# Layer 1 of a four-layer network: where y starts, who adds the scan's steps, and who applies the third norm's factor

## The chip, the cores and the metric

The kernel runs on one core of one Trainium2 chip. The metric is the device time of one launch in microseconds (us), the median of several runs. A core has a matrix engine (PE, TensorE), a vector engine (DVE, VectorE), an activation engine (ACT, ScalarE), a general engine (POOL, GpSimd) and a queue engine (SP) that here issues DMAs. They run beside each other, and each works through its own instructions strictly in the order in which the program lists them.

## The reference

An input of 16 images, 96 channels, 56 x 56 pixels (L = 3136) goes through four layers. Layer 0 is a masked convolution block; layers 2 and 3 are Fourier mixers with an MLP. The change touches layer 1 alone, a selective scan over the image in four directions:

```python
u = _ln(z, norm1_g, norm1_b) @ in_proj_w.T
uc = silu(depthwise_conv3x3(u))                      # 192 channels
xs = [rows, columns, rows reversed, columns reversed] # of uc
dts, Bs, Cs = split(einsum('bkdl,kcd->bkcl', xs, x_proj_w))
dt = softplus(dt_projs_w @ dts + dt_projs_b)
a  = exp(dt * A);  bb = dt * Bs * xs
h  = scan(h = a * h + bb)                            # along L, in each direction
y  = h * Cs + Ds * xs
ym = sum of the four directions, turned back into the image
z  = z + _ln(ym, out_norm_g, out_norm_b) @ out_proj_w.T   # second norm
m  = _ln(z, norm2_g, norm2_b)                             # third norm
z  = z + gelu(m @ fc1_w.T + fc1_b) @ fc2_w.T + fc2_b
```

## The kernel before

Layer 1 is the function `layer1`. For each image it has six generators (L1495 to L1530), which run as tasks beside each other for different images:

- `normed` (L1065) and `front` (L1097): first norm, projection into 192 channels, the 3 x 3 convolution as matmuls with diagonal taps into PSUM tiles `p_c` (L1170), eviction by ACT (L1191), Silu (L1193), the small projection `p_x` (L1207). The 192 channels of an image lie in two tiles of 128 partitions: `u0` holds the first 128; `um` holds the other 64 twice, once by rows and once by columns.
- `made_of` (L1220): for twelve units per image (six combinations of tile and direction, two halves each) and two steps of 784 columns per unit, PE makes `p_d` (L1237), ACT turns it into `dt` (exponential L1244, logarithm L1246) and `a` (exponential, L1253). `rows_of` loads the rows of B and C, spread over partitions, as `bc` (L1266).
- `scanned` (L1274): per step of 784 columns, DVE multiplies `dt` by `u` (L1325) and by B into the PSUM tile `driven` (L1328), scans (`TENSOR_TENSOR_SCAN`, L1334 backward and L1336 forward), and, one step later in `finish`, multiplies the state by C into `hc` (L1289). For units 0 and 2, the first of each tile, DVE then starts the output, `y = dsum * u + hc` (L1292). For the other four units GpSimd adds `hc` to y (L1358), in `sums` (L1341). In the end DVE adds the turned half of `ym` to the other (L1363).
- `back` (L1368): statistics of y and the second norm, then for seven groups of 448 pixels: output projection, DVE's `z` (L1428, L1432), squares on ACT (L1438), sums on DVE (L1440 to L1443), GpSimd's power -1/2 giving the third norm's factor `r` (L1445), DVE's product `zn = z * r` (L1447), transposition on PE (L1451), then the MLP (L1461, L1463, L1471) and the sum (L1474). Three chains of groups run side by side.

The order of each engine's queue is not written by hand. Each generator yields an `Op` with an engine and a cost before it issues that piece of work, and `in_order` (L276) plays all tasks against modelled engines: of all waiting pieces it issues the one with the lowest start time plus a lead. The leads stand in `TUNED` by engine and generator; an ACT piece that needs another function table also gets `hold` added. A piece can take buffers (`take`), free them (`give`), wait for a time that another has posted, and post one. Which piece follows which thus comes from the costs, leads and buffer counts; on the chip the order is then fixed. What an `Op` covers is issued in one piece, such as the nine taps of a convolution block:

```python
yield pe(9, 0.66, ())
for k in range(9):
```

The tiles `u0`, `um` and the two y of an image come from a list of seven (`big`).

Of the kernel before, what the change touches and what calls it, by code (L numbers as in the profile page):

```python
# [23 lines left out]
T = 448  # L24
NT = L // T
ROWS = T // S
Q = 112
# [32 lines left out]
def packed(x):  # L60
# [96 lines left out]
    for m in (C, DIN):  # L157
# [21 lines left out]
                        'z': 2,  # L179
                        'zn': 1,  # L180
                        'zt': 1,
                        'hid': 1,
                        'xr': 2},
            'leads': {('PE', 'spreads'): -2.2,
                      ('PE', 'steps'): -3.4,
                      ('SP', 'sums'): -1.2,
                      ('ACT', 'spreads'): -0.3,
                      ('DVE', 'additions'): -0.2,
                      ('ACT', 'hidden'): -0.7,
                      ('SP', 'norms'): 0.7,  # L190
                      ('POOL', 'fronts'): -4.6,
                      ('DVE', 'some'): -0.3,
                      ('POOL', 'norms'): 0.4,
                      ('PE', 'some'): -0.6,
                      ('ACT', 'sums'): 0.5,
                      ('SP', 'projected'): -1.4,
                      ('DVE', 'norms'): 0.1,
                      ('POOL', 'backs'): -0.6,
                      ('POOL', 'additions'): -1.3,
                      ('PE', 'projected'): 0.7,  # L200
                      ('DVE', 'backs'): -1.8,
                      ('ACT', 'fronts'): -0.2,
                      ('PE', 'fronts'): -2.4,
                      ('DVE', 'spreads'): -0.8,
                      ('SP', 'rows_of'): 0.2},
            'hold': 0.7,
            'norm': -6,
# [679 lines left out]
def layer1(ctx, tc, src, given, dst, flags=None, soft=False):  # L887
# [151 lines left out]
    def pe(n, each, take=("ps",), give=(), **k):  # L1039
        return Op("PE", 1.05 * n * each, 0.25, take, give, **k)  # L1040

# [55 lines left out]
    def front(b, it):  # L1097
# [60 lines left out]
        def convolved(j):  # L1158

            pad, u = (whole, halves)[j], us[j]  # L1160
            for c in range(0, (8, 4)[j], 2):
                yield Op("none", 0.0, 0.0, take=("ps",))
                p = pair("p_c")
                yield pe(9, 0.66, ())
                for k in range(9):
                    for b in range(2):
                        r0 = 7 * (c + b) + k // 3
                        for s in range(2):
                            to = (s ^ b) * 64
                            nc.tensor.matmul(  # L1170
                                p[to : to + 64, b, :TC], taps[64 * s : 64 * s + 64, j, k],
                                pad[64 * s : 64 * s + 64, r0 : r0 + 7, k % 3 : k % 3 + S],
                                start=k == 0, stop=k == 8,
                            )
                at = TC * c
                if j == 0:
                    outs = [
                        (u[:, at : at + TC], p[:, 0, :TC], TC),
                        (u[:64, at + TC : at + 2 * TC], p[64:, 1, :TC], TC),
                        (u[64:, at + TC : at + 2 * TC], p[:64, 1, :TC], TC),  # L1180
                    ]
                else:
                    outs = []
                    for s, b in ((0, 0), (0, 1), (1, 0), (1, 1)):
                        to, row = (s ^ b) * 64, HALF_S * s + 7 * (c + b)
                        own = p[to : to + 64, b, :TC]
                        outs.append((u[:64, S * row : S * row + TC], own, TC))
                        outs.append((turned(u[64:])[:, row : row + 7], own.rearrange("p (h w) -> p h w", w=S), 1.7 * TC))
                for i, (out, in_, cost) in enumerate(outs):
# [11 lines left out]
        for b in range(2):  # L1201
            yield pe(3, 0.7, ("ps",) if b == 0 else ())
            p = pair("p_x") if b == 0 else p
# [16 lines left out]
    def made_of(it):  # L1220
# [4 lines left out]
        def steps():  # L1225

            for unit in units:
                i, h = unit
                order = (0, 1) if i < 3 else (1, 0)
                for s in order:  # L1230
# [11 lines left out]
                    else:  # L1242
                        yield act(SUB, give=("ps",), table="exp")
                        nc.scalar.activation(flat, p[:, :, :TC], AF.Exp, bias=dtb[:, i : i + 1])  # L1244
                        yield act(SUB, table="exp")
                        nc.scalar.activation(dt, dt, AF.Ln, bias=one)  # L1246
# [3 lines left out]
                for s in order:  # L1250
                    give = ("proj",) if last and s == order[1] else ()
                    yield act(SUB, give=give, table="exp", post=times[unit, s])
                    nc.scalar.activation(a[:, SUB * s : SUB * s + SUB], made[unit][s], AF.Exp, scale=aneg[:, i : i + 1])  # L1253
# [20 lines left out]
    def scanned(it):  # L1274
# [4 lines left out]
        def scan():  # L1279
            y0, ym = None, None  # L1280
            before, late = None, None

            def finish(unit, s, a, t, end, out, own_u):
                i = unit[0]
                yield dve(
                    SUB, take=("hc",), give=("bc",) + (("a",) if end else ()), post=None if i in (0, 2) else added[unit, s]
                )
                made[unit]["hc", s] = hc = buf([P, SUB], "hc")
                nc.vector.tensor_tensor(hc, a, t[:, 1], ALU.mult)  # L1289
                if i in (0, 2):  # L1290
                    yield dve(SUB, give=("hc",), post=added[unit, s])
                    nc.vector.scalar_tensor_tensor(  # L1292
                        out, own_u, dsum[:, i // 2 : i // 2 + 1], hc, ALU.mult, ALU.add
                    )

            for unit in units:
# [3 lines left out]
                u = um if mixed else u0  # L1300
                if unit in ((0, 0), (2, 0)):
                    yield Op("none", 0.0, 0.0, take=("big",))
                    y = big.pop(0)
                    if mixed:
                        ym = y
                    else:
                        y0 = y
                    it["y"].append(y)
                y = ym if mixed else y0
                for s in ((1, 0) if back else (0, 1)):  # L1310
# [9 lines left out]
                    free = end and i in (4, 5)  # L1320
                    yield dve(SUB, 1.85e-3 if flip else 1.04e-3, wait=times[unit, s], give=("big",) if free else ())
                    if free:
                        big.append(u)
                    dt, a = made[unit][s], made[unit]["a"][:, SUB * s : SUB * s + SUB]
                    nc.vector.tensor_tensor(as_own(dt), as_own(dt), own(u), ALU.mult)  # L1325
                    yield dve(SUB, wait=bct[unit, s], give=("dt",))
                    t, b = bcs[unit, s][0], driven[:, :SUB]
# [9 lines left out]
                    before = None if end else (a[:, 0:1] if back else a[:, SUB - 1 : SUB], last_sub)  # L1337
                    late = (unit, s, a, t, end, own(y), own(u))
            yield from finish(*late)

        def sums():  # L1341
            for unit in units:
                i, h = unit
                back = i >= 3
                if i in (0, 2):
                    continue
                for s in ((1, 0) if back else (0, 1)):
                    at = HALF * h + SUB * s
                    yield Op("none", 0.0, 0.0, wait=added[unit, s])
                    y, u = it["y"][i == 5], (um if i == 5 else u0)  # L1350
                    hc = made[unit]["hc", s]
# [3 lines left out]
                    else:  # L1355
                        out = y[:, at : at + SUB]
                    yield Op("POOL", 1.9, give=("hc",))
                    nc.gpsimd.tensor_tensor(out, out, hc, ALU.add)  # L1358
            ym = it["y"][1]
            for g in range(4):  # L1360
                yield dve(L / 4, 1.85e-3)
                own = image(ym[:64])[:, 14 * g : 14 * g + 14]
                nc.vector.tensor_tensor(own, own, turned(ym[64:])[:, 14 * g : 14 * g + 14], ALU.add)  # L1363

        it["sums"] = sums()
        yield from scan()

    def back(b, it):  # L1368
# [38 lines left out]
        def group(g):  # L1407
# [16 lines left out]
            for q in range(4):  # L1424
                nc.tensor.matmul(p[:Q, 4 + q, :C1], each(x, q), rows[0], start=True, stop=True)
            yield dve(4 * C1, take=("z",))
            z = buf([Q, 4, C1], "z")
# [15 lines left out]
            nc.vector.tensor_scalar(v, v, 1.0 / C, EPS, ALU.mult, ALU.add)  # L1443
            yield Op("POOL", 1.4)
            nc.gpsimd.tensor_tensor(r, v, nhalf[:, :4], ALU.pow)  # L1445
            yield dve(4 * C)
            nc.vector.tensor_tensor(zn, z, r.unsqueeze(2).to_broadcast([Q, 4, C]), ALU.mult)  # L1447
            yield pe(4, 0.1, ("ps", "zt"), ("zn",))
# [9 lines left out]
            def hidden(j):  # L1458
                yield pe(1, 0.75, ("ps",), ("zt",) if j == 2 else ())
                p = pair("p_f")  # L1460
                nc.tensor.matmul(p[:, 0, :T], w_fc1[:, P * j : P * j + P], zt, start=True, stop=True)  # L1461
                yield act(T, table="gelu", give=("ps",))
                nc.scalar.activation(hid[:, j], p[:, 0, :T], AF.Gelu, bias=b_fc1[:, j : j + 1])  # L1463
# [22 lines left out]
    def item():  # L1486
        lists = lambda: {(k, s): [] for k in units for s in range(2)}
        return {
            "y": [], "left": NT, "ready": [], "normed": [], "done": [], "begun": [], "made": {k: {} for k in units},
            "times": lists(), "bcs": lists(), "bct": lists(), "added": lists(),  # L1490
        }
# [472 lines left out]
```

## Time and profile before

| | |
|---|---|
| median of 3 runs | 7093.66 us (7093.59 to 7100.32) |
| profiled execution, its own time | 7093.59 us |
| its span in the profile | 7091.7 us |
| layer 1 in it | 1152.6 to 4401.8 us |
| busy in layer 1 (3249.2 us) | PE 2708.5, DVE 2618.9, ACT 2320.4, POOL 948.7 us |
| L1292, all of it (DVE) | 128 instructions, 132.2 us |
| L1447, all of it (DVE) | 112 instructions, 142.5 us |
| L1358, all of it (POOL) | 256 instructions, 528.3 us |

In the profile, a group's line gives the source line, engine, operation, output and inputs with shapes, the count, then the busy time and the mean length in ns of one, then how long the engine was idle just before such instructions and for whom it waited. A timeline line begins with the start and the length in us, and ends with the idle time in brackets. PEclk is the share of its full clock that PE was granted.

### The profile page before, as it was taken

The numbers are of one execution on the slowest core, as the hardware profiler recorded it, in microseconds if no ns is written. First come the engines' busy times: TensorE is split into PE (matmuls) and PEld (weight loads), VectorE is DVE, ScalarE is ACT, GpSimd is POOL, SyncE is SP. The second block draws the span as 40 slices with busy tenths as digits, with TensorE's granted clock in tenths as the row PEclk, the third lists the DMA queues.
The fourth block names the chain that finished last, engine by engine and source line by source line (L and its number), as shares of the span: only waits on it lengthen the run. The fifth ranks groups of instructions, "written<-read, shape, count | busy, mean of one in ns | idle before, by whom it ended". The sixth has DMA issues, their size and how long they took to land. (4 is left out here: it accounts for less than half of the span.)

```text
span 7091.7 us, 113066 instructions
## 1 busy us (share of the span) xinstructions
PE 6092.5 (86%) x45643; PEld 4183.4 (59%) x45643; DVE 5440.8 (77%) x7075; ACT 4521.6 (64%) x5897; POOL 1377.5 (19%) x898
## 2 busy tenths in 40 slices
PE   7999997888888888888888866788999989999986
PEld 3444443345445455555544444787888888888875
DVE  6786884598888888888888894667777777777775
ACT  4454542677777777777777762455666666666664
POOL 0000000233332323233332231111111111111110
PEclk9999997788898898888888867899999999999997
DMA  1111111444444444444544342445555455555542
GB/s 38 32 38 34 38 33 52 132 143 134 131 137 132 136 133 138 130 138 135 140 131 126 110 128 64 97 107 123 130 116 128 111 130 119 123 134 118 120 105 62
DMA packets 508374, 763.72 MB, mean 108 GB/s; under 512 B 206337, under 2 KB 339137, under 8 KB 504530
## 3 DMA queue, kind: packets, MB, share of 16 engines
q1 hardware_dynamic: 506818, 753.53, 41.2%
q8 instruction: 363, 5.95, 0.4%
q0 software_dynamic: 1024, 2.85, 0.1%
q14 instruction: 169, 1.38, 0.1%
HBM read 563.65 MB, written 192.59 MB: 107 GB/s over the span
## 5 line engine op out<-in xcount | busy, mean ns | idle before, releaser
L1664 POOL TENSOR_TENSOR r<-v,nhalf 112x16 f32<-112x16 f32 (+1 forms) x128 | 392.9, 3076 | 2238.8 <-DVE v L1662 1677.2
L1358 POOL TENSOR_TENSOR big<-big,hc 128x784 f32<-128x784 f32 x256 | 528.3, 2064 | 1139.4 <-DVE hc L1289 1131.3
L1325 DVE TENSOR_TENSOR dt<-dt,big 128x784 f32<-128x784 f32 x384 | 500.6, 1304 | 249.4 <-ACT a L1253 249.1
L827 DVE SCALAR_TENSOR_TENSOR h<-pad,rows,h 128x1568 f32<-128x1568 f32 x288 | 525.9, 1844 | 3.9
L1244 ACT ACTIVATE dt<-p_d,l_dtb 128x784 f32<-128x784 f32 x384 | 350.3, 912 | 183.0 <-PE p_d L1237 157.8
L1237 PE MATMUL p_d<-proj,l_dt 32*128 32x392 f32 x1536 | 382.8, 581 | 93.5 <-ACT big L1191 52.4
L1461 PE MATMUL p_f<-zt,w_fc 96*128 96x448 f32 x672 | 401.7, 731 | 41.9 <-ACT zt L1454 27.8
L1471 PE MATMUL p_g<-l_fc,hid 128*112 128x96 f32 x2688 | 425.5, 304 | 11.7 <-ACT hid L1463 11.0
L1722 PE MATMUL p<-k_f,z 112*128 112x112 f32 x3072 | 375.0, 282 | 67.5 <-DMA z<-d 57.9
L1722 PEld LDWEIGHTS p<-k_f,z 112*128 112x128 f32 x3072 | 370.6, 199 | 76.3 <-issue 57.9
L1471 PEld LDWEIGHTS p_g<-l_fc,hid 128*112 128x112 f32 x2688 | 385.4, 219 | 41.0 <-ACT hid L1463 30.8
L1770 PE MATMUL p_v<-w,gg 128*112 128x97 f32 x2048 | 377.9, 267 | 34.5 <-DVE gg L1759 11.6
L1170 PE MATMUL p_c<-x,taps 64*64 64x392 f32 x4608 | 400.8, 497 | 0.8 <-ACT big L1191 0.8
L1328 DVE TENSOR_TENSOR drive<-dt,bc 128x784 f32<-128x784 f32 x384 | 387.8, 1010 | 10.2
L1771 PE MATMUL p_v<-w2both,gg 128*112 128x97 f32 x2048 | 376.0, 266 | 0.0
L1289 DVE TENSOR_TENSOR hc<-a,bc 128x784 f32<-128x784 f32 x384 | 371.8, 968 | 3.4 <-POOL big L1358 3.4
L1246 ACT ACTIVATE dt<-dt,one 128x784 f32<-128x784 f32 x384 | 363.4, 946 | 8.5
L1691 PE MATMUL p_a<-first,xt 97*112 97x192 f32 x1792 | 336.6, 336 | 18.1 <-ACT xt L1685 9.0
L1334 DVE TENSOR_TENSOR_SCAN a<-a,drive 128x784 f32<-128x784 f32 x192 | 350.3, 1825 | 0.0
L1336 DVE TENSOR_TENSOR_SCAN a<-a,drive 128x784 f32<-128x784 f32 x192 | 350.2, 1824 | 0.0
L1253 ACT ACTIVATE a<-dt,aneg 128x784 f32<-128x784 f32 x384 | 347.5, 937 | 2.7 <-DVE a L1334 1.4
L800 PE MATMUL p_c<-pad,taps 64*64 64x392 f32 x4032 | 347.4, 494 | 0.3 <-ACT pad L782 0.3
(341 smaller groups left out, 14838.7 us busy)
## 6 DMA issues: line engine op xcount, KB each, us to landing
bc<-bc SPq DMA_DIRECT2D x256, 784.0 KB
bc<-bc SPq DMA_DIRECT2D x256, 392.0 KB
d<-y SPq DMA_DIRECT2D x448, 192.0 KB
z<-d SPq DMA_DIRECT2D x128, 672.0 KB
d<-uu SPq DMA_DIRECT2D x256, 169.8 KB
z<-d SPq DMA_DIRECT2D x192, 194.0 KB
xc<-x SPq DMA_DIRECT2D x96, 336.0 KB
x<-in_x SPq DMA_DIRECT2D x16, 1176.0 KB
```

The lines of the kernel that those rows point to most:

```text
L827: nc.vector.scalar_tensor_tensor(out, view, taps9[:, i : i + 1], out, ALU.mult, ALU.add)
L1170: nc.tensor.matmul(p[to : to + 64, b, :TC], taps[64 * s : 64 * s + 64, j, k], pad[64 * s : 64 * s + 64, r0 : r0 + 7, k % 3 : k % 3 + S], s ...
L1237: nc.tensor.matmul(p[:, b, :TC], wdt[on, i], proj[on, h], start=True, stop=True)
L1325: nc.vector.tensor_tensor(as_own(dt), as_own(dt), own(u), ALU.mult)
L1328: nc.vector.tensor_tensor(b, dt, t[:, 0], ALU.mult)
L1358: nc.gpsimd.tensor_tensor(out, out, hc, ALU.add)
L1461: nc.tensor.matmul(p[:, 0, :T], w_fc1[:, P * j : P * j + P], zt, start=True, stop=True)
L1471: nc.tensor.matmul(p[:Q, q, :C], hid[:, j, own], fc2[:, j], start=j == 0, stop=False)
L1664: nc.gpsimd.tensor_tensor(r, v, nhalf[:, :n], ALU.pow)
L1722: nc.tensor.matmul(p[:, q, :Q], flat[:, P * (3 * q + k) : P * (3 * q + k) + P], f2, start=True, stop=True)
L1770: nc.tensor.matmul(out, gs[2 * h][:, at + k], w["w2"][:, 2 * h], start=True, stop=False)
L1771: nc.tensor.matmul(out, gs[1][:, at + k], w["w2both"][:, h], start=False, stop=True)
```

## The change

Five things change in `layer1`, and with them the planned order of all queues:

- y begins as `dsum * u` on ACT: four new instructions of 1568 columns per image, in a new generator `inits` that runs beside the scan. The first tile's y is made at the start, the second's after a step of unit 4. The count `uses` decides when a `u` tile returns to the list.
- DVE's L1292 goes; GpSimd adds `hc` for all six units instead of four.
- The taps of a convolution block are announced to the planner in three pieces of three.
- The third norm's factor is applied to z by GpSimd, behind its power, and `zn` has two buffers.
- Costs, leads and `hold` (0.7 to 0.0) of the planner have other values.

```diff
-                        'zn': 1,
+                        'zn': 2,
...
-            'leads': {('PE', 'spreads'): -2.2,
+            'leads': {('PE', 'spreads'): -0.9,
                       ('PE', 'steps'): -3.4,
-                      ('SP', 'sums'): -1.2,
+                      ('SP', 'sums'): 1.2,
...
-                      ('POOL', 'fronts'): -4.6,
+                      ('POOL', 'fronts'): -6.6,
...
-                      ('PE', 'fronts'): -2.4,
...
+                      ('ACT', 'inits'): 0.7,
+                      ('PE', 'hidden'): -2.0,
+                      ('POOL', 'some'): -0.9,
...
-            'hold': 0.7,
+            'hold': 0.0,
...
     def pe(n, each, take=("ps",), give=(), **k):
-        return Op("PE", 1.05 * n * each, 0.25, take, give, **k)
+        return Op("PE", 1.1 * n * each, 0.25, take, give, **k)
...
                 p = pair("p_c")
-                yield pe(9, 0.66, ())
                 for k in range(9):
+                    if k % 3 == 0:
+                        yield pe(3, 0.66, ())
...
                 nc.vector.tensor_tensor(hc, a, t[:, 1], ALU.mult)
-                if i in (0, 2):
-                    yield dve(SUB, give=("hc",), post=added[unit, s])
-                    nc.vector.scalar_tensor_tensor(
-                        out, own_u, dsum[:, i // 2 : i // 2 + 1], hc, ALU.mult, ALU.add
-                    )
...
         def sums():
             for unit in units:
                 i, h = unit
                 back = i >= 3
-                if i in (0, 2):
-                    continue
                 for s in ((1, 0) if back else (0, 1)):
                     at = HALF * h + SUB * s
                     yield Op("none", 0.0, 0.0, wait=added[unit, s])
+                    yield Op("none", 0.0, 0.0, wait=it["begins"][i in (2, 5), h])
...
-                    yield Op("POOL", 1.9, give=("hc",))
+                    yield Op("POOL", 2.1, give=("hc",))
                     nc.gpsimd.tensor_tensor(out, out, hc, ALU.add)
...
+        def inits():
+            for j, u in enumerate((u0, um)):
+                if j:
+                    yield Op("none", 0.0, 0.0, wait=added[(4, 1), 1])
+                yield Op("none", 0.0, 0.0, take=("big",))
+                y = big.pop(0)
+                it["y"].append(y)
+                for h in range(2):
+                    yield act(HALF, post=it["begins"][j, h])
+                    cols = slice(HALF * h, HALF * h + HALF)
+                    nc.scalar.activation(y[:, cols], u[:, cols], AF.Identity, scale=dsum[:, j : j + 1])
+                it["uses"][j] -= 1
+                if it["uses"][j] == 0:
+                    big.append(u)
+                    yield Op("none", 0.0, 0.0, give=("big",))
+
         it["sums"] = sums()
-        yield from scan()
+        yield [scan(), inits()]
...
-            yield Op("POOL", 1.4)
+            yield Op("POOL", 1.6)
             nc.gpsimd.tensor_tensor(r, v, nhalf[:, :4], ALU.pow)
-            yield dve(4 * C)
-            nc.vector.tensor_tensor(zn, z, r.unsqueeze(2).to_broadcast([Q, 4, C]), ALU.mult)
+            yield Op("POOL", 1.1)
+            nc.gpsimd.tensor_tensor(zn, z, r.unsqueeze(2).to_broadcast([Q, 4, C]), ALU.mult)
```

## The prediction

> **What bounds the kernel now.** I began with the 40 slices of the page, to find the stage that the change touches.
>
> ```profile
> PE   7999997888888888888888866788999989999986
> DVE  6786884598888888888888894667777777777775
> ACT  4454542677777777777777762455666666666664
> POOL 0000000233332323233332231111111111111110
> PEclk9999997788898898888888867899999999999997
> ```
>
> A slice is 177 us. Slices 8 to 24 are layer 1 (first instruction at 1152.6 us, last at 4401.8): PE and DVE both stand at 8 of 10, ACT at 7, POOL at 2 or 3. Nobody is full, so averages won't tell. The timeline shows DVE beginning the scans of an image every 190.4 us (1834.4, 2024.8, 2215.9, 2404.4, 2594.8 ...). I cut one such period in two where the second of DVE's two long waits ends, and asked for busy times by window:
>
> ```profile
> 2403.90:2464.80 60.90, 51.38 (x565) 22.93 (x562) 40.18 (x41) 51.58 (x67) 12.10 (x14) 0.92 0.33 109
> 2464.80:2594.30 129.50, 112.47 (x701) 71.18 (x699) 123.02 (x138) 94.38 (x118) 46.68 (x26) 0.87 0.53 147
> ```
>
> Columns: length, then busy us of PE, weight loads, DVE, ACT, POOL, then clock, DMA share and GB/s. The halves have different limits. **Part A** (60.9 us, the convolution of the next image): DVE 66%, PE and ACT 84 and 85%. **Part B** (129.5 us, most of the scans beside norms, projections and the MLP): DVE 95%, PE 87%, ACT 73%. So B is DVE's, and A belongs to PE and ACT feeding each other. Next the groups and waits of ten periods (1834.4 to 3738.3; divide by ten):
>
> ```profile
> L1325 DVE TENSOR_TENSOR dt<-dt,big 128x784 f32<-128x784 f32 x240 | 314.0, 1308 | 163.3 <-ACT a L1253 163.3
> L1447 DVE TENSOR_TENSOR zn<-z,r 112x384 f32<-112x384 f32 x70 | 93.9, 1342 | 13.2 <-POOL r L1445 13.2
> L1292 DVE SCALAR_TENSOR_TENSOR big<-big,dsum,hc 128x784 f32<-128x784 f32 x80 | 82.6, 1033 | 2.1
> L1358 POOL TENSOR_TENSOR big<-big,hc 128x784 f32<-128x784 f32 x160 | 329.1, 2057 | 715.6 <-DVE hc L1289 713.4
> L1445 POOL TENSOR_TENSOR r<-v,nhalf 112x4 f32<-112x4 f32 x70 | 111.3, 1590 | 376.2 <-DVE v L1443 375.4
> L1451 PE MATMUL p_t<-ident,zn 112*96 112x112 f32 x280 | 50.4, 315 | 103.1 <-DVE zn L1447 103.1
> ```
>
> The change strikes L1447 and L1292 from DVE. L1447 is dear for its size: 1.34 us, where an addition of about the same shape (L1432) takes 0.56. The timeline tells why:
>
> ```profile
> 2480.33 2.22 POOL L1358 TENSOR_TENSOR big<-big,hc 128x784 f32<-128x784 f32 x1
> 2480.39 2.58 DVE L1447 TENSOR_TENSOR zn<-z,r 112x384 f32<-112x384 f32 x1 [0.91 <-POOL r L1445]
> ```
>
> DVE stands until GpSimd's addition is over and only then multiplies (0.55 us when undisturbed, at 2513.82). PE pays twice: L1451 waited 10.3 us per image for zn.
>
> [...] the scans, reading `driven` in PSUM, should be free (1.84 us beside an addition, and as much without). [...] The trace shows a clock of 0.67 over 2464.8 to 2485.0, where the first two zn waits lie, and 1.00 over 2545 to 2565, so PE's busy time would fall a little with its waits.
>
> **The change, part by part, per image.**
>
> (1) DVE loses 8 of L1292 (8 x 1.03 = 8.3 us) and 7 of L1447 (7 x 1.34 = 9.4). Four of the eight L1292 lie in A (2408.9 to 2435.3), where DVE waits anyhow: worth nothing. B is relieved of 9.4 + 4.1 = 13.5.
>
> (2) GpSimd gains 8 additions. L1358 takes 1.85 contiguous, 2.23 turned, and units 0 and 2 are contiguous: 14.8 us. It gains 7 multiplications of 384 elements: 1.85/784 x 384 = 0.9 each, 6.3 us. From 58.9 to 80 us of about 182: not a bound by itself. Locks: an addition starts when `hc` ends and the 1.8 us scan covers it, leaving 0.15 for the next L1325 (1.10 at 2449.82 against 0.95): 4 in B, 0.6 us. A multiplication comes at any time. DVE instructions with two SBUF inputs fill about 47% of the time (L1325, L1328, L1289, L1125 and L1363 together)[...]; I charge half its length, 7 x 0.45 = 3.2 us. Bounds: 0 (always under a scan or when DVE waits) and 7 x 2.0 = 14 (standing as long as L1447 did). B's DVE net: 13.5 - 3.8 = 9.7.
>
> (3) ACT gains 4 scalings of 1568 columns. No row has them; L1253 (a scale from a column, 784) takes 0.937[...], 6.4 in all. Identity runs between exponentials without a table load (L1134 at 2502.42). In B ACT has 35 us free; in A only 9. I put half in A: +3.2 us of ACT. Below: none in A; above: all, +6.4.
>
> (4) The 72 matmuls of a convolution block, 6.2 to 6.8 us in one piece, go in three pieces of 2. DVE's waits of 7.13 us (2431.45) and 8.91 us (2464.83) for `a` are in A: `p_d` stood behind such blocks, then dt, logarithm and `a`. It costs no instruction, but holds a PSUM pair longer where others come between. Bounds: A down to ACT's own 51.6 + 3.2 = 54.8 (-6), or up by the scalings and a missing pair (+3). I take -1.5.
>
> (5) `hold` 0.7 to 0 can split gelus from each other. ACT loads tables 16 times a period (1.283 us each). Two more cost 2.6 us, hidden in B's ACT slack; with seven more pairs (18 us) that cover would be used up. I take none on the path. A second `zn` buffer only removes a wait. The new leads reorder every queue, SP's too: `bc`, `xc`, `xr`, `root` loads. DMA engines are 47% busy, and DVE waits 163.3 of its roughly 270 idle us per ten periods for `a`, almost none for DMA, so I count nothing; if the cover is gone, one late `bc` is a DVE wait of a few us per image, which is in the upper end.
>
> **The sum.** B would be 129.5 - 9.7 = 119.8 if DVE alone counted, but PE has 112.5 of work there, 94%. PE becomes the next limit; at 92% B takes 122.2, so -7. With A -1.5: -8.5 per image, 16 x 8.5 = 136 us. The profiled execution took 7093.59 (span 7091.7); the median of the runs is 7093.66, the same. 7093.6 - 136 = 6958.
>
> **Rivals.**
> - *PE takes over at once*: its 26 us of waits per image merely change their cause and give back 2 us: -32, 7062. For: PE and DVE stand level at 86%. Against: 10.3 us of those waits are zn's.
> - *Everything opens*: `p_d` slips between taps, A falls by 6, B by 10[...]: -16, 6838. For: DVE's two long waits in A. Against: ACT, 6.4 us heavier.
> - *Slower*: GpSimd's queue, in order, puts each multiplication before or behind an addition[...]; `hc` has one buffer, so an addition held by the 6.1 us power (L1093) also stops DVE. B has 11 added GpSimd instructions; from 13.5/11 = 1.23 us of DVE stall each the gain is gone, and at 1.64 (18 us) it is +4.5 per image: 7166. For: L1447 itself stood 2.0 us. Against: the additions of today cost L1325 0.1 to 0.6.
> - *It does not do it*: the planned order differs from what the chip needs, saved work turns to waits: about 7093.
>
> **How the numbers follow.** Main case (-85 to -200) 0.58, everything opens 0.13, PE at once (-15 to -85) 0.15: faster 0.86. No change 0.04, slower 0.10; 0.2% is 14 us, about what a measurement here can tell from no change. Range 6850 to 7075: it holds the main case and most of its neighbours. Bounds: A -6 to +3, locks 0 to 14.
>
> **What would show it.** L1447 becomes POOL, 112 instructions near 0.9 us; L1358's group 384; L1292 gone; 64 ACT Identities near 1.6 us. Right: periods near 182 us, DVE busy near 150 of them, PE above 88%, L1451's wait well under 10 us, L1325's wait for `a` under 16. Wrong: L1325, L1328 or L1289 lengthened by over 10 us per image, DVE waiting on L1358 for `hc`, more than 20 table loads a period, or periods over 190.

## The result and the profile after

The changed kernel took 7015.44 us (median, 7007.49 to 7021.21) beside 7096.99 for the kernel before on the same chip: ratio 0.9878, 95% interval 0.9861 to 0.9895, about 82 us faster. The forecast was 6958, or 136 us.

The slices of the page of the changed kernel, one of them now 175 us:

```profile
PE   7999997788888888888888776889999989899986
DVE  6886885488888888888887892667777777777775
ACT  4455553678888888888887762556666666666664
POOL 0000000244444444444444442111111111111110
PEclk9999998888998988998889767899999999999997
```

In layer 1 GpSimd rises from 2 or 3 tenths to 4, ACT from 7 to 8; PE and DVE stay at 8. So no engine was freed visibly, and none became full. Layer 1 runs from 1151.5 to 4313.4 us, 3161.9 against 3249.2 before: -87.3 us, the whole of the gain. Its edges give nothing (the first scan 5.3 us later, the last scan interval 20.9 shorter, the tail after it 15.3 longer). The 15 intervals from the first scan of one image to that of the next hold it: 87.0/15 = 5.8 us each on average. Ten of them by window, the kernel before and then the changed one (length, then busy us of PE, weight loads, DVE, ACT, POOL, then clock, DMA share, GB/s):

```profile
1834.40:3738.30 1903.90, 1644.74 (x12592) 950.75 (x12590) 1632.66 (x1782) 1459.45 (x1839) 589.16 (x400) 0.88 0.47 134
```

```profile
1822.90:3666.10 1843.20, 1617.46 (x12593) 935.52 (x12592) 1559.69 (x1631) 1520.32 (x1880) 825.20 (x550) 0.90 0.48 139
```

Per period: 190.4 became 184.3; PE's busy time fell by 2.7 us and its idle time by 3.3; DVE's busy time fell by 7.3 and its idle time rose by 1.2. DVE's saving was larger than the gain and was partly turned into waiting. I cut a changed period at the same instruction as in the prediction, the ninth L1325 (now L1310) of an image:

```profile
2375.80:2426.30 50.50, 43.87 (x526) 20.12 (x526) 37.90 (x38) 44.41 (x64) 18.97 (x10) 0.95 0.36 120
2426.30:2560.10 133.80, 117.86 (x737) 73.47 (x737) 117.96 (x126) 107.71 (x126) 63.49 (x46) 0.88 0.52 146
```

Part A is 50.5 us in all ten changed periods, against 57.8 to 60.5 (mean 58.6) before; part B is 133.8 against a mean of 131.8. Part B, where DVE was relieved, became longer. But PE does 44 us of work in A where it did 51: 7.5 us of its work moved over into B. The parts trade work under a new plan, and only their sum means something.

Groups of the changed kernel over those ten periods:

```profile
L1310 DVE TENSOR_TENSOR dt<-dt,big 128x784 f32<-128x784 f32 x240 | 320.7, 1336 | 127.4 <-ACT a L1257 126.4
L1318 DVE TENSOR_TENSOR drive<-dt,bc 128x784 f32<-128x784 f32 x240 | 276.1, 1150 | 5.5
L1446 DVE SCALAR_TENSOR_TENSOR v<-z 112x4 f32<-112x4 f32 x70 | 45.6, 651 | 0.0
L1347 POOL TENSOR_TENSOR big<-big,hc 128x784 f32<-128x784 f32 x240 | 487.5, 2031 | 738.0 <-DVE hc L1290 688.3 <-DMA bc<-bc 31.0 <-ACT big L1386 14.2
L1452 POOL TENSOR_TENSOR zn<-z,r 112x384 f32<-112x384 f32 x70 | 95.0, 1362 | 2.4
L1364 ACT ACTIVATE big<-big,dsum 128x1568 f32<-128x1568 f32 x40 | 62.6, 1588 | 0.0
L1456 PE MATMUL p_t<-ident,zn 112*96 112x112 f32 x280 | 53.0, 326 | 44.4 <-POOL zn L1452 44.4
L1456 PEld LDWEIGHTS p_t<-ident,zn 112*96 112x96 f32 x280 | 32.8, 153 | 99.2 <-POOL zn L1452 77.0 <-issue 22.2
```

DVE's wait for `a` fell from 16.3 to 12.6 us per image. `drive` (L1328, now L1318) rose from 0.994 to 1.150 us, and L1446 (before L1441), an instruction of 112 x 4 elements that took 0.154 before, now takes 0.651. The two in the kernel before, over its ten periods:

```profile
L1328 DVE TENSOR_TENSOR drive<-dt,bc 128x784 f32<-128x784 f32 x240 | 238.6, 994 | 6.5
L1441 DVE SCALAR_TENSOR_TENSOR v<-z 112x4 f32<-112x4 f32 x70 | 10.8, 154 | 0.0
```

The timeline of the changed kernel shows both standing for GpSimd (start, length; the pairs alone):

```profile
2448.51 3.45 POOL L1347 TENSOR_TENSOR big<-big,hc 128x784 f32<-128x784 f32 x1
...
2449.90 2.90 DVE L1318 TENSOR_TENSOR drive<-dt,bc 128x784 f32<-128x784 f32 x1
...
2497.66 2.24 POOL L1347 TENSOR_TENSOR big<-big,hc 128x784 f32<-128x784 f32 x1 [3.75 <-DVE hc L1290]
...
2497.89 2.03 DVE L1446 SCALAR_TENSOR_TENSOR v<-z 112x4 f32<-112x4 f32 x1
```

The first addition ends at 2451.96, and L1318 only at 2452.80: nearly all of its own 0.98 us (the median of its 240) came after the addition. The second ends at 2499.90 and L1446 at 2499.92. The multiplication has left DVE, and the blocking has passed to other DVE instructions that run beside GpSimd.

### The profile page after: what moved, and what is told of

The parts are those of the page before. It is cut to its first block, busy times and chain, and to the rows that moved or that the text cites. A ratio compares the mean times of both kernels' runs of the same rounds, so it can differ in the third digit from the quotient of the medians.

```text
span 7005.7 us, 113387 instructions
## 1 busy us (share of the span) xinstructions
PE 6047.5 (86%) x45643; PEld 4148.8 (59%) x45643; DVE 5315.5 (76%) x6835; ACT 4617.9 (66%) x5959; POOL 1746.8 (25%) x1138
## 5 line engine op out<-in xcount | busy, mean ns | idle before, releaser
L1347 POOL TENSOR_TENSOR big<-big,hc 128x784 f32<-128x784 f32 x384 | 776.3, 2022 | 1243.6 <-DVE hc L1290 1184.3
L1310 DVE TENSOR_TENSOR dt<-dt,big 128x784 f32<-128x784 f32 x384 | 517.3, 1347 | 198.6 <-ACT a L1257 197.2
L1466 PE MATMUL p_f<-zt,w_fc 96*128 96x448 f32 x672 | 374.9, 704 | 85.1 <-ACT zt L1459 68.6
L1241 PE MATMUL p_d<-proj,l_dt 32*128 32x392 f32 x1536 | 392.8, 594 | 60.4 <-ACT hid L1468 36.4
L1318 DVE TENSOR_TENSOR drive<-dt,bc 128x784 f32<-128x784 f32 x384 | 430.2, 1120 | 9.3
L1174 PE MATMUL p_c<-x,taps 64*64 64x392 f32 x4608 | 426.2, 501 | 11.7 <-ACT big L1195 9.1
L1476 PE MATMUL p_g<-l_fc,hid 128*112 128x96 f32 x2688 | 393.8, 291 | 0.9 <-ACT hid L1468 0.9
L1476 PEld LDWEIGHTS p_g<-l_fc,hid 128*112 128x112 f32 x2688 | 358.3, 207 | 18.3 <-issue 10.7
```

The source lines that it names most:

```text
L1174: nc.tensor.matmul(p[to : to + 64, b, :TC], taps[64 * s : 64 * s + 64, j, k], pad[64 * s : 64 * s + 64, r0 : r0 + 7, k % 3 : k % 3 + S], s ...
L1241: nc.tensor.matmul(p[:, b, :TC], wdt[on, i], proj[on, h], start=True, stop=True)
L1318: nc.vector.tensor_tensor(b, dt, t[:, 0], ALU.mult)
L1476: nc.tensor.matmul(p[:Q, q, :C], hid[:, j, own], fc2[:, j], start=j == 0, stop=False)
```

## The experiments

Periods are means of ten, from scan start to scan start; A and B are cut as above. "Steps" is the period over 3.4133 us: in the traces of both kernels PE's granted clock is either 1.0 or 0.5, and every stretch of either, but the last of each trace, lasts a whole number of these (the expectations call them windows).

| kernel | ratio to before | period | steps | A + B | DVE busy | PE busy |
|---|---|---|---|---|---|---|
| before | 1 | 190.4 | 55.8 | 58.6 + 131.8 | 163.3 | 164.5 |
| changed | 0.9878 | 184.3 | 54.00 | 50.5 + 133.8 | 156.0 | 161.7 |
| changed, product on DVE | 0.9907 | 184.3 | 54.00 | 51.6 + 132.7 | 155.9 | 163.1 |
| before, product on GpSimd | 1.0064 | 193.5 | 56.7 | 60.4 + 133.1 | 159.6 | 164.4 |
| changed, y on DVE | 0.9971 | 187.9 | 55.0 | 49.6 + 138.3 | 157.7 | 165.1 |
| before, y on ACT | 1.0221 | 201.8 | 59.1 | 53.7 + 148.1 | 154.8 | 171.6 |
| changed, taps in one | 1.0213 | 201.4 | 59.0 | 67.2 + 134.2 | 152.2 | 169.7 |
| before, taps in pieces | 1.0160 | 199.6 | 58.5 | 52.0 + 147.6 | 161.6 | 169.7 |
| old work, new plan values | 1.0464 | 221.9 | 65.0 | 48.5 + 173.3 | 162.4 | 177.9 |
| new work, old leads | 0.9924 | 188.1 | 55.1 | 62.2 + 125.9 | 151.2 | 165.0 |
| changed, PE relieved | 0.9793 | 179.5 | 52.6 | 49.5 + 130.0 | 155.1 | 156.5 |
| changed, rows added on DVE | 0.9907 | 184.3 | 54.00 | 49.1 + 135.2 | 160.0 | 160.4 |

PE's matmuls are the same in every row but the last two, yet its busy time runs from 161.7 to 177.9 us. It goes with the granted clock, which over ten periods was 0.90 in the changed kernel, 0.88 in the kernel before, 0.83 with the taps in one and 0.81 with the old work under the new plan values. In the changed kernel four `p_d` matmuls took 0.93 us at a clock of 1.00 (2405.74 us) and 1.67 at 0.50 (2477.95).

### The product, put back and moved alone

From the changed kernel, every queue in its order (only DVE and GpSimd exchange one instruction):

```diff
-            nc.gpsimd.tensor_tensor(zn, z, r.unsqueeze(2).to_broadcast([Q, 4, C]), ALU.mult)
+            nc.vector.tensor_tensor(zn, z, r.unsqueeze(2).to_broadcast([Q, 4, C]), ALU.mult)
```

> The changed kernel with one word altered: the product zn = z * r is issued on DVE again, at the same place in the planned order, so every other instruction of every queue keeps its place. Theory (moved work): DVE pays 7 products per image of 0.55 to 1.9 us, 4 to 13 us, and gets back what the product on GpSimd cost it in locks (3 to 4 us): periods 2 to 6 us longer than 184.3, 7045 to 7110 us. Rival (the new order made the gain, the place of the product is of no account): within 15 us of 7015.

It took 7029.98 us (7020.71 to 7034.93), ratio 0.9907 (0.9886 to 0.9928), an interval that overlaps that of the changed kernel: the rival's case, by a hair. Its period is the same 184.3 us, and DVE is busy 155.9 us of it: seven products came back to DVE at 0.644 us each, and about as much blocking went. So the product's move takes nothing from DVE in this order. The reverse edit on the kernel before, in its order:

> The kernel before with one word altered: the product zn = z * r is issued on GpSimd, at the same place in the planned order; all else keeps its place. Theory of the prediction (the scan stretch is DVE's, each product there costs 1.34 us): DVE busy falls by about 9.4 us less 3.2 us of locks, periods by 4 to 7 us, 6990 to 7040 us. Rival, from the run with the product back on DVE (what the product gives DVE it takes back in locks): DVE busy within 3 us of 163.3 per image, 7075 to 7110 us. Second rival (GpSimd holds the product behind an addition and PE waits for it): over 7110.

It took 7148.19 us, ratio 1.0064 (1.0041 to 1.0087): slower, as the second rival had it. DVE's busy time fell by 3.7 us per image, less than half of the 9.4 that it was relieved of, and close to seven undisturbed products of 0.55 us (3.9). PE waited longer. The kernel before first, then this one, ten periods each (of L1451's weight loads and matmuls):

```profile
L1451 PEld LDWEIGHTS p_t<-ident,zn 112*96 112x96 f32 x280 | 32.9, 149 | 141.7 <-issue 53.2 <-DVE zn L1447 31.9 <-ACT a L1253 27.0
```

```profile
L1451 PE MATMUL p_t<-ident,zn 112*96 112x112 f32 x280 | 53.3, 328 | 129.6 <-POOL zn L1447 129.6
L1451 PEld LDWEIGHTS p_t<-ident,zn 112*96 112x96 f32 x280 | 34.2, 154 | 165.0 <-POOL zn L1447 152.0 <-issue 12.5
```

The last field is the idle time before the instructions and for whom. Loads waited 3.2 us per image for zn and now 15.2, matmuls 10.3 and now 13.0 (the two rows run beside each other, so these don't add up). A product takes 1.42 us on GpSimd there; the shortest in the changed kernel took 0.83. In that order the product trades DVE's time for PE's waiting.

### The start of y, put back and moved alone

The changed kernel with `y = dsum * u + hc` on DVE for units 0 and 2 and without `inits`, planned anew:

> The changed kernel with y begun on DVE as before (units 0 and 2 by the fused multiply-add, no scalings on ACT, GpSimd adds four units), everything else as changed, planned anew. Theory (moved work): DVE +8.3 us per image less some 2 to 3 us of locks, ACT -6.4: periods 2 to 5 us longer, 7045 to 7095 us. Rival 1 (the gain is the order's or the product's): 7000 to 7030. Rival 2 (the scalings on ACT cost more than DVE saved): under 7000.

It took 7076.58 us, ratio 0.9971 (0.9960 to 0.9983): about 61 us of the 82 are gone. The ten periods run from 184.6 to 190.6. But DVE did not pay 8.3 us: it is busy only 1.7 us more, for with eight GpSimd additions fewer much blocking went too (`drive` is back at 0.994, the small instruction at 0.393). PE is busy 3.4 us more, at a clock of 0.88, which is nearly the whole longer period, and DVE's waits for `p_g` rose from 6.9 to 17.7 us. This run plans anew, so it prices the part together with the order that it brings. The same part alone, on the kernel before:

```diff
-                if i in (0, 2):
-                    yield dve(SUB, give=("hc",), post=added[unit, s])
-                    nc.vector.scalar_tensor_tensor(
-                        out, own_u, dsum[:, i // 2 : i // 2 + 1], hc, ALU.mult, ALU.add
-                    )
...
-        yield from scan()
+        yield [scan(), inits()]
```

> The kernel before with y begun on ScalarE and all steps added by GpSimd; the third norm's product stays on DVE, the taps in one piece, leads, hold and costs those of before. Theory A (taking L1292 off DVE is the part that saves, whatever the plan): DVE is busy 6 to 8 us less per image, the period falls by 3 to 5 us, 7015 to 7055. Theory B (PE's queue and its half-clock windows set the period unless the plan is fitted to the new work): DVE's busy time falls as much, but its waits for a grow by what it loses; 7085 to 7250, periods at or above 190 us.

It took 7250.34 us, ratio 1.0221 (1.0195 to 1.0248), Theory B's side. DVE's busy time fell by 8.5 us to 154.8, less than in the changed kernel, and the period still grew to 201.8. DVE's waits for `a` rose from 16.3 to 20.0 us per image, those for `p_g` from 5.0 to 10.4. A lighter DVE was worth nothing here: PE was busy 171.6 us instead of 164.5, at a clock of 0.85 instead of 0.88, and waited more.

### The taps, put back and moved alone

The changed kernel with the block announced in one piece:

```diff
+                yield pe(9, 0.66, ())
                 for k in range(9):
-                    if k % 3 == 0:
-                        yield pe(3, 0.66, ())
```

> The changed kernel with the nine taps of a convolution block announced in one piece again. Theory (the pieces let p_d through, DVE's wait for a in the convolution stretch shrinks from 16.3 to 12.6 us per image): periods 2 to 4 us longer, DVE's wait for a back near 16 us, 7040 to 7080 us. Rival (the pieces do nothing; the wait shrank by the leads): 7005 to 7030.

It took 7242.52 us, ratio 1.0213 (1.0192 to 1.0233), far beyond what either theory had. The clock over ten periods is the lowest of these orders but one, and DVE is nearly the least busy:

```profile
1846.30:3860.70 2014.40, 1697.27 (x12438) 977.13 (x12440) 1522.45 (x1632) 1513.84 (x1874) 811.54 (x550) 0.83 0.45 127
```

Part A is 67.2 us, longer than in the kernel before (58.6). What the pieces do is seen on PE. The kernel before, then the changed one (PE's timeline, excerpts):

```profile
2425.72 0.93 PE L1237 MATMUL p_d<-proj,l_dt 32*128 32x392 f32 x4
2426.58 6.16 PE L1170 MATMUL p_c<-x,taps 64*64 64x392 f32 x72
...
2435.40 0.93 PE L1237 MATMUL p_d<-proj,l_dt 32*128 32x392 f32 x4 [1.20 <-ACT big L1191]
```

```profile
2399.72 0.93 PE L1241 MATMUL p_d<-proj,l_dt 32*128 32x392 f32 x4
2400.57 2.21 PE L1174 MATMUL p_c<-x,taps 64*64 64x392 f32 x24
2402.71 0.58 PE L1083 MATMUL p_s<-xc,ones 96*32 96x224 f32 x8
...
2403.60 2.21 PE L1174 MATMUL p_c<-x,taps 64*64 64x392 f32 x24
2405.74 0.93 PE L1241 MATMUL p_d<-proj,l_dt 32*128 32x392 f32 x4
```

From one `p_d` to the next PE needed 9.7 us where it now needs 6.0: small pieces of other work go between the taps. Of DVE's two waits for `a` in A, 7.13 and 8.91 us, 6.47 and 1.42 are left. But the pieces alone, under the leads of before:

> The kernel before, with the nine taps of a convolution block given to the planner in three pieces of three, and nothing else; leads, hold and costs are those of before. Theory (the parts fit one another: the changed kernel with its taps in one piece took 7242.5, the old work under the new leads 7420.5): the pieces alone gain nothing, and a re-planned queue with old leads is as likely slower: 7090 to 7300, periods of 190 to 205 us. Rival (the pieces are a gain of their own, because p_d slips between them and dt's waits of 7 to 9 us for a in part A shrink): 7010 to 7080, dt waiting less than 14 us per image for a, periods of 187 us or less.

took 7210.05 us, ratio 1.0160 (1.0136 to 1.0184). Part A did shrink, to 52.0 us, and DVE waits for `a` only 9.9 us per image; B grew to 147.6. The rival was right on A and wrong on the sum.

### The plan's values

The work of before (taps in one, y and product on DVE) under the new leads, `hold` and costs:

> The kernel before with the changed leads, hold and costs of the planner, and none of the moved work (product and units 0 and 2 on DVE, taps in one piece, one zn buffer). Theory (moved work makes the gain): no faster than 7097, and more likely slower by 20 to 80 us since these leads were made for other work. Rival (the plan makes the gain): 7015 to 7050.

It took 7420.47 us, ratio 1.0464 (1.0442 to 1.0485), with periods of up to 293 us: 328 us slower, where 20 to 80 were the likelier case. The reverse, the new work and costs under the old leads and `hold`:

> The changed kernel's work and costs under the leads and hold of before. Theory B (the leads are fitted to the work): slower than the changed kernel by over 30 us, 7050 to 7300, the period no longer the same in every image. Rival (the new work alone makes the gain, the leads are of no account): within 20 us of the changed kernel, 6995 to 7035, period 184.3 us.

It took 7040.84 us, ratio 0.9924 (0.9901 to 0.9946): some 59 us of gain without the new leads, and about 25 more with them (33 by the two ratios). Both theories missed: the new leads are worth something, but most comes with the work and the costs. Nor was the period irregular: seven in a row took 187.7 us. DVE is busier in the changed kernel (156.0) than here (151.2), because blocking depends on the order. Under the old leads, over ten periods, `drive` is as before:

```profile
L1315 DVE TENSOR_TENSOR drive<-dt,bc 128x784 f32<-128x784 f32 x241 | 241.3, 1001 | 6.1 <-DVE v L1404 0.2
```

and the period is 3.8 us longer all the same. Each part alone made the kernel before slower, and together they made it faster. New costs alone under the old work and leads were not run, nor was the second `zn` buffer alone. Why each part alone is slower is not shown beyond the waits given above.

### What sets the changed period

Three edits in the changed kernel's order, one engine each. First DVE: the variance is rearranged so that one of its three instructions goes and the one that was blocked (L1446) reads PSUM. ACT makes the row sum that the new instruction needs.

```diff
-            nc.vector.scalar_tensor_tensor(v, s1, -1.0 / C, s1, ALU.mult, ALU.mult)
-            nc.vector.tensor_tensor(v, v, s2, ALU.add)
+            nc.vector.scalar_tensor_tensor(v, q1, -1.0 / C, s2, ALU.mult, ALU.add)
```

> The changed kernel in the same planned order, with the third norm's variance made without an instruction that has two SBUF inputs: ACT squares z with its row sum (388 columns instead of 384), DVE's sum of squares goes to a free corner of the PSUM tile driven, and one fused instruction takes the place of two (L1446 and L1447, 0.65 + 0.16 us). If DVE's locks hold the period: DVE busy falls by 4 to 5 us per image and the period with it, by 3 to 5 us: 6935 to 6970 us. If PE and its clock windows of 3.413 us set the period: DVE busy falls all the same, the period stays 184.3 = 54 windows or steps to 53 windows (180.9): 7015 or about 6965, and nothing between.

It took 7008.70 us, ratio 0.9866 (0.9850 to 0.9882), the same as the changed kernel. DVE's busy time fell by only 1.2 us per image, where 4 to 5 were expected:

```profile
L1450 DVE TENSOR_SCALAR v<-v 112x4 f32<-112x4 f32 x70 | 38.3, 547 | 2.4
L1449 DVE SCALAR_TENSOR_TENSOR v<-zn,drive 112x4 f32<-112x4 f32 x70 | 11.1, 159 | 2.4
```

The fused instruction runs free at 0.159 us, and the next one, with a single SBUF input, stands in its place (0.170 in the changed kernel): the long ones end some 25 ns after a GpSimd addition that had begun before them, as those of L1446 in the changed kernel do (12 to 27 ns). With 1.2 us taken off, this run says little on what a DVE lighter by several us would give.

Then ACT, which leaves out most of the columns of the scaling that starts y (from the second use of a buffer on only 196 columns of each half):

> The changed kernel in the same planned order, leaving out part of the computation on ACT: from the third image on, the scalings that begin y cover 196 of 1568 columns each (0.45 us instead of 1.59; 4.6 us per image less), the rest of y begins with what the tile held. If ACT's scalings are on the path: periods down by 2 to 5 us, 6940 to 6985 us. If they lie beside other work, as the prediction had it for all but half: within 15 us of 7015, periods 184.3.

It took 7015.33 us, ratio 0.9877 (0.9858 to 0.9897), with ACT busy 4.3 us less per image. No gain: in this order the scalings cost nothing that shows. Then PE, which leaves out the four matmuls a group that add the layer's input and the offsets to the MLP's output:

```diff
-                nc.tensor.matmul(p[:Q, q, :C], each(x, q), rows[1][:, :C], start=False, stop=True)
```

> The changed kernel in the same planned order, leaving out part of the computation on PE: the 4 matmuls per group that add layer 1's own input to the MLP's sum (L1477, 10.75 us of PE busy per image); the output lacks that addend. If PE sets the period: down by 7 to 11 us per image, 6850 to 6910 us, and to a whole number of 3.413 us windows (52 or 51: 177.5 or 174.1). If DVE or ACT sets it: under 3 us per image, 6970 to 7015.

It took 6954.36 us, ratio 0.9793 (0.9775 to 0.9811), 61 us below the changed kernel. Ten periods of each of the two:

```profile
1822.80:3666.00 1843.20, 1617.23 (x12592) 935.17 (x12592) 1559.29 (x1631) 1477.68 (x1880) 825.29 (x550) 0.90 0.48 139
```

```profile
1822.80:3618.20 1795.40, 1565.11 (x12038) 880.20 (x12030) 1550.62 (x1631) 1517.79 (x1880) 822.97 (x550) 0.89 0.50 142
```

Relief of ACT (first line) leaves the window at 1843.20 us to the last digit. Relief of PE by 5.2 us a period shortens it by 4.8. Neither theory had that: the one for PE expected 7 to 11 us and a period of 52 or 51 whole steps, the one for DVE or ACT under 3. PE's idle time stayed (22.6, now 23.0 us), while DVE's fell from 28.4 to 24.5. The edit also shortens the chain through `p_g`, for which DVE waited 6.9 us and now 3.3; the run doesn't separate that from PE's amount of work.

That digit is the second thing. The clock changes in steps of 3.413 us, and equal periods are a whole number of these: 184.32 = 54.00 steps in the changed kernel and in all edits of its order except this one; 187.73 = 55.00 in the runs of equal periods under the old leads; 191.15 = 56.00 in the frequent period of before. In the changed kernel the half-clock stretches begin 45.5, 79.6, 96.7, 130.8 and 158.1 us after an image's first scan, in all ten images, 11 steps in all. With PE relieved the periods are 177.9 to 180.8 us, repeating every five images, and five make 897.7 us, 263.00 steps. That periods stand at whole numbers is what the runs show; that the clock's steps hold them there is my reading, and no run tested it alone. If it is so, an edit of one or two us may show nothing at all, and the unchanged periods with DVE or ACT relieved don't prove that these engines are off the path.

### A candidate

The last kernel keeps PE's relief and computes the whole result: DVE adds the input and the offsets in two more additions of 112 x 384 per group. It also has the variance of the first edit above, and makes the product in place.

> A candidate to beat both, in the changed kernel's order: layer 1's input and the row of offsets are no longer added to the MLP's output by PE's four matmuls a group (28 an image) but on DVE, ahead of the sum that it makes anyhow: two additions of 112 x 384 a group, 14 an image, one with a PSUM input, about 0.55 us each, +7.7 us of DVE per image beside -5.2 us of PE (that is what leaving those matmuls out took from PE's busy time). The variance is made from sums in PSUM, the product is made in place. Theory (PE sets the period and DVE has 28 us a period free): near the kernel that left the matmuls out (6954): 6940 to 6985, periods near 179.5 us. Rival (DVE's spare time lies at the wrong places, the added instructions come in front of scans): 7000 to 7060, periods at 184.3 us or above.

It took 7025.33 us (7021.29 to 7045.33), ratio 0.9907 (0.9880 to 0.9934), no better than the changed kernel; the rival was right.

```profile
1830.30:3673.60 1843.30, 1603.57 (x12035) 901.11 (x12038) 1600.21 (x1701) 1515.70 (x1881) 817.56 (x550) 0.86 0.48 139
```

DVE is busy 4.0 us more per period than in the changed kernel. PE, with as many matmuls fewer as in the relieved kernel, is busy 160.4 us instead of 156.5, at a clock of 0.86 instead of 0.89: 15 half-clock steps in a typical period, where the relieved kernel had 10 to 13. Three or four steps of 3.4 us at half speed, some 6 us, can cost PE that time (an estimate). PE did not wait longer for DVE itself (6.8 us, with PE relieved 7.4), but GpSimd waited 22.7 us for DVE's variance where it had waited 16.0, and PE 9.3 for GpSimd's product where it had waited 6.0. So the theory that PE sets the period is too simple. My reading is that PE and DVE set it together, and that PE's relief counts only while DVE doesn't slow the chain that feeds PE. No run in this order took as much from DVE as the relieved kernel took from PE, so DVE's own share is not measured.

## Why the prediction was right in direction and too large

The gain of 82 us lies inside the stated range but just outside the main case (85 to 200), in the band that the prediction gave to "PE takes over at once" with a chance of 0.15. The direction and the two limits were right; what follows shows that the number came about partly in another way, so it is in part luck that it lies this near.

**What bounds, and the cut in A and B.** Both engines as limits was right; the split was not. Forecast: B -7, A -1.5. Measured: A -8.1, B +2.0. The bound for A (-6 to +3) was exceeded, and PE's work left A for B (51 us in A before, 44 after); new work under old leads had A +3.6 and B -5.9. A cut inside a period is no wall for a planner that reorders all queues.

**(1) DVE's relief** was smaller than the removed busy times. For L1292, putting it back costs 61 of the 82 us, but DVE is busy only 1.7 us more, and the cost shows in PE's time; alone on the old plan the move took 8.5 us from DVE and made the kernel slower. For L1447, DVE's 1.34 us were about 0.6 of work and 0.7 of standing for GpSimd, and standing isn't removed with the instruction: in the new order its move gave DVE nothing, in the old one 3.7 of 9.4 us. The cross-check was in the prediction: 0.55 undisturbed.

**(2) Locks**, DVE standing for GpSimd, is a term of the sum that was mis-sized. The charge was 3.8 us per image. Measured from the means of the groups: `drive` 24 x 0.156 = 3.7, `dt` and `hc` 1.3, L1446 7 x 0.497 = 3.5, `xn` 4 x 0.145 = 0.6, L1094 0.5: 9.6 us, inside the bounds of 0 to 14. Only long instructions with two SBUF inputs had been counted as victims, an assumption that no trace had shown; 4.0 of the 9.6 fell on tiny ones, L1446 and L1094 (1.24 us against 0.70 before, with one SBUF input). DVE's busy time fell by 7.3 instead of 17.7 - 3.8 = 13.9. The product takes 1.36 us in place of 0.9 (0.83 at best), the additions 2.03. With 9.6 in place of 3.8 the forecast's own sum gives 125.6 us for B and -5.4 in all (an estimate, which puts all of the 9.6 in B), near the -6.1 measured for the period. But this term doesn't explain the difference by itself: with DVE 4.8 us lighter, under the old leads, the kernel was slower than the changed one.

**(3) ACT**: 1.588 us, 6.3 us per image, against 1.6 and 6.4, an estimate of which the kernel before showed only the 0.937 of L1253. The charge of half of it in A was not seen: leaving most of the scalings out left the time as it was (with the caution above on whole steps).

**(4) The taps** were priced at -1.5 us. Their removal costs 227 us, and alone the pieces cost 111. So they have no price of their own: what they give depends on the rest of the plan.

**(5) Hold, leads, loads, DMA**: ACT loads tables 16 times a period, as before, and none of DVE's waits is put down to a DMA before or after, so nothing was the right charge for these. For the order it was not: the new leads and `hold`, counted as nothing, are worth 25 to 33 us with the new work, and together with the new costs they made the old work 328 us slower.

**The sum.** That PE becomes the limit was the right idea. B was to have PE at 92%; it has 117.86 of 133.8 us, 88%, as it also does more work there. Over the whole period the forecast of -8.5 us was to come out of PE's idle time, 25.9 us; of this only 3.3 came, and 2.7 more from its busy time, which the prediction had let fall "a little" without a figure. The waits changed their cause: for zn the matmuls wait 4.4 us instead of 10.3, but the weight loads 7.7 instead of 3.2, and at p_f the waits for `zt` rose from 1.4 to 4.4. That is the first rival's mechanism at part strength: -5.8 us in 15 intervals instead of -8.5 in 16. Of the signs for "right", DVE's wait for `a` (12.6, under 16) and the matmuls' wait for zn came; PE at 87.7% just missed its 88, and periods (184.3, not 182), DVE's busy time (156, not 150) and the product on GpSimd (1.36, not 0.9) were off.

**The slower rival** had the right agent. DVE lost 9.6 us for 15 added GpSimd instructions, 0.64 each, half of its threshold of 1.23. On the old order it came true for the product alone, through PE's loads and not through DVE.

What stays open: how much of the 59 us without leads belongs to the costs, what a DVE lighter by several us in this order would give, and whether a period could leave 54 steps by any edit smaller than PE's.

## What to carry to other kernels

Price a busy time by the undisturbed instruction before you count its removal as a saving: the time that it stood for another engine can pass to its neighbour. Where a planner orders the queues, parts that are each slower alone can be faster together, so test a part both by taking it out and by putting it in alone. Look for equal periods to the last digit before you read an edit without effect as proof that its engine is off the path.

## What the runs showed of the hardware

- Steady periods of the loop over images stood at whole numbers of the 3.413 us step in which PE's clock changed between 1.0 and 0.5: 54.00, 55.00, 56.00, and 263.00 for five in a row.
- The blocking by GpSimd strikes instructions of 112 x 4 elements as hard as long ones: up to 2.03 us for one of 0.16. A `tensor_scalar` with one SBUF input is struck too (L1450 with the variance rearranged, 0.547 on average against 0.170).
- A GpSimd power over 112 x 28 took 4.8 to 5.5 us (in the kernel before up to 6.1). An addition queued behind one began at 2420.51 us in the changed kernel, and L1318, begun 0.04 us later, took 2.63 us.
- In layer 1 of the changed kernel DVE began its 2659 instructions, and ACT its 2753 (table loads aside), in exactly the order in which the program lists them.
